# Attention over 4096 tokens: the denominators of a round and two output projections share one exchange of three PSUM banks at the 14th tile of keys

## The chip, the core and the metric

The kernel runs on one core of one Trainium2 chip, in one launch. The metric is the device time of an execution in microseconds (us); less is better. Engines are named as in the profile: PE is TensorE's matmul, PEld its weight load, DVE is VectorE, ACT is ScalarE, POOL is GpSimd, SP is SyncE (here it only issues DMAs). L1860 is line 1860 of the kernel before.

## What is computed

A small network on one image of 256 channels, 64 x 64 pixels: a convolution-like layer of windowed linear attention, then softmax attention over all 4096 pixels as tokens, then a mixture of 8 experts of which each token uses two. The change lies in the softmax attention:

```python
def _L1_attn_ref(x, w_qkv, b_qkv, w_out, b_out):
    b, n, d = x.shape                      # 1, 4096, 256
    h = 8; dh = d // h; scale = d ** (-0.5)
    q, k, v = split(x @ w_qkv + b_qkv)     # 8 heads of 32
    dots = jnp.einsum('bhid,bhjd->bhij', q, k) * scale
    attn = jax.nn.softmax(dots, axis=-1)
    out = jnp.einsum('bhij,bhjd->bhid', attn, v)
    return out @ w_out + b_out
...
t = t + _L1_attn_ref(_ln_t(t), ...)
t = t + _L1_ffn_ref(_ln_t(t), ...)         # logits, top 2 of 8, gelu experts
```

Everything is float32.

## The kernel before, in words

**Stages.** The first layer takes the span to about 960 us, the queries, keys and values to 1065, the attention stage to about 2163, the experts the rest, with the output at the end.

**The attention stage** works on transposed scores: keys lie on the 128 partitions, 512 queries along a row. A *round* r is one chunk of 512 queries (qc, 8 of them) and one group of four heads (g, 2 of them): 16 rounds, r = 0 to 15, the two groups of a chunk one after the other. A round goes over NT = 32 *tiles* i of 128 keys. One pass of the loop at L1982 is a *step*, one tile of one round:

- `scores` (L1848) makes the scores of four heads: the first head goes into a bank called "one" (a single buffer), heads 2 to 4 into a set of three banks called "three" (two buffers, L1814). [...] ScalarE takes the exponential of "one" (L1869) and then of "three" (L1872) into one of eight SBUF buffers of 4 x 512.
- `value_sums` (L1894) multiplies the weights of the tile two steps back by the values, summing over the round in "acc" (L1819, four heads side by side in the columns of the array). At the end of a round `take` copies the sums to the result (L1904).
- `add` (L1889) sums the exponentials of the tiles on VectorE (L1892), into the buffer of the round's first tile; every fourth tile from the sixth on is instead added to the second tile's buffer by an accumulating DMA on POOL's queue (`moved`, L1880). `gather` (tile 5 of the next round, L1912) joins the two sums.

Tiles are counted from 0 below and in the code, so the 14th tile is i = 13.

**The denominators** of round r-1 are handled during round r. `pack` (i = 9) takes a set of "three", sums the joined sums over the partitions by a multiplication with ones (L1919, recorded at L1819 with `ones` among its operands), and ScalarE copies the result to SBUF (L1922); SP writes four rows to DRAM (L1924) and reads them back spread over the partitions (L1925). `turn` (i = 17) takes reciprocals (L1932), writes them (L1933) and broadcasts each head's row to 32 partitions (four DMAs, L1936). `spread` (i = 29) multiplies the result of the round by them (L1943).

**The projections.** A tile of 128 tokens of the result is multiplied by w_out, together with 8 columns for the router's logits (L1794, 264 columns; `project`, L1791), added to the residual t by VectorE (L1798) and its mean and variance taken (L160, L161). `some_projections` (L1973) takes a set of "three" for two tiles. It is called at i = 13 and 25 of the rounds of the second group from round 3 on: 14 calls, 28 of 32 tiles; the last four come after the loop (L2022).

A use of a set of "three" by `pack` or `some_projections`, between the scores of two tiles, is called an *exchange* here.

**The early routing** of the first 12 tiles of tokens is cut into small VectorE operations with planned costs (L1088 to L1198). L1952 to L1968 distribute them over places (r, i) of rounds 8 to 14, each with so much room. Two of the pieces are matmuls: `count` (L1126) and `invert` (L1167). They use the third bank of an exchange of projections (`shared`, L1962) and are issued ahead of the projections; VectorE copies their results (L1130, L1177) after the additions of L1798.

**What sets the order.** The order in which things are written, readiness as the builder estimates it, and orders that are written by hand: `tc.issue_after(x)` puts an instruction behind x on its engine. ScalarE's copy in `pack` is behind the current exponential of "three" (L1921) and the next exponential is behind that copy (L1868). `work_on` (L2006) starts the loads of the first two experts at i = 0 and 29 of the last round, behind the last broadcast of `turn`. The list `free` (L1842) decides which of the eight buffers a tile gets: the one that is due free first, where `pack` frees the round's sum with due time NT(r + 1) + 11 (L1927).

Of the kernel before, what the change touches and what calls it, by code (L numbers as in the profile page):

```python
# [31 lines left out]
C = 256  # L32
KC = C // P
N = 4096
NT = N // P
# [5 lines left out]
NB = IMG // BH  # L41
# [5 lines left out]
NE = 8  # L47
# [73 lines left out]
def tile_conv_attn_hybrid(ctx: ExitStack, tc: tile.TileContext, a: dict, out: bass.AP):  # L121
# [62 lines left out]
    early = act[:, :, 3 * N // 4 : 3 * N // 4 + 3 * C + NE]  # L184
# [37 lines left out]
    def tok(i):  # L222
        return slice(P * i, P * (i + 1))
# [44 lines left out]
    with ExitStack() as phase:  # L268
# [406 lines left out]
        def packed(jobs):  # L675

            steps = []
            for job in jobs:
                if not steps or sum(j[0] for j in steps[-1]) + job[0] > CH:
                    steps.append([])  # L680
                steps[-1].append(job)
            return steps
# [359 lines left out]
    def all_of(ops):  # L1042
        for op in ops:
            op()
# [169 lines left out]
    with ExitStack() as phase:  # L1214
# [15 lines left out]
        with (  # L1230
# [55 lines left out]
            def turn(c):  # L1286
                for i in range(NB * c, NB * (c + 1)):
                    hn = work.tile([P, C], F32, name="hn", bufs=4) if c else first_rows(i)
                    if c:
                        norm.apply(hn, i)  # L1290
                    to_channels(hn, act[:, :, tok(i)], ps)

                    nc.gpsimd.tensor_add(t[:, i, :C], t[:, i, :C], bo)
# [497 lines left out]
        def project(prs, tiles, result, then=None):  # L1791
            for pr, i in zip(prs, tiles):
                for k in range(KC):
                    nc.tensor.matmul(  # L1794
                        pr[:, : C + NE], result(k, i), wo[:, k, :], start=k == 0, stop=k == KC - 1
                    )
            for pr, i in zip(prs, tiles):
                nc.vector.tensor_add(t[:, i, :], pr[:, : C + NE], t[:, i, :])  # L1798
            if then:
                then()  # L1800
            for i in tiles:
                found = norm2.stats(i)
            return found

        with tc.If(tame > 0) as branch:
            with (
# [6 lines left out]
                def three_banks():  # L1813
                    return ps.tile([P, 3, CH], F32, tag="three", name="ps_three", bufs=2)  # L1814
# [21 lines left out]
                result = lambda g, qc: act[:, 0, CH * (2 * g + qc % 2) : CH * (2 * g + qc % 2 + 1)]  # L1836
                buffers = [work.tile([P, 4 * CH], F32, name=f"pe{n}") for n in range(5)]
                buffers += [act[:, k, 4 * CH * n : 4 * CH * (n + 1)] for k, n in ((0, 1), (1, 0), (1, 1))]
                own, other = 0, 1
                by_dma = range(5, NT, 4)  # L1840
                head = lambda z, hd: z[:, CH * hd : CH * (hd + 1)]
                free = [(-1, n) for n in range(len(buffers))]  # L1842
# [3 lines left out]
                weights_of, acc_of, sums_of, emptied = {}, {}, {}, []  # L1846
# [42 lines left out]
                def add(r, i):  # L1889
                    if i not in (own, other) and not moved(r, i):  # L1890
                        total = buffers[sums_of[r, own]]
                        latest[:] = [nc.vector.tensor_add(total, total, weights_of[r, i]).ins]  # L1892

                def value_sums(r, i):  # L1894
                    (qc, g), pe = rounds[r], weights_of.pop((r, i))
                    if i == 0:
                        acc_of[r] = ps.tile([P, CH], F32, tag="acc", name="ps_acc")
                    values = lambda hd: v[:, i, P * g + D * hd : P * g + D * (hd + 1)]
                    per_head(acc_of[r], values, lambda hd: head(pe, hd), i == 0, i == NT - 1)
                    return pe  # L1900

                def take(r, copy):
                    qc, g = rounds[r]
                    return copy(result(g, qc), acc_of.pop(r))  # L1904

                def by_ones(to, weights, start, stop):
                    per_head(to, lambda hd: ones, lambda hd: head(weights, hd), start, stop)

                def gather(r):
                    total, moved_total = (buffers[sums_of[r, i]] for i in (own, other))  # L1910
                    with tc.issue_after(latest[0]):
                        nc.vector.tensor_add(total, total, moved_total)  # L1912
                    free.append((NT * (r + 1) + 8, sums_of[r, other]))

                held, latest, turned = [], [], []

                def pack(r):
                    den = three_banks()[:, 0]
                    by_ones(den, buffers[sums_of[r, own]], True, True)  # L1919
                    rec = work.tile([P, CH], F32, tag="rec", name="rec")  # L1920
                    with tc.issue_after(emptied[0]):  # L1921
                        emptied.append(nc.scalar.copy(rec, den).ins)  # L1922
                    some = work.tile([P, CH // D], F32, name="some")
                    nc.sync.dma_start(dens, rec[::D, :])  # L1924
                    nc.sync.dma_start(some, packed(dens))  # L1925
                    held.append(some)
                    free.append((NT * (r + 1) + 11, sums_of[r, own]))  # L1927

                def turn():
                    some = held.pop()  # L1930
# [9 lines left out]
                def spread(r):  # L1940
                    qc, g = rounds[r]
                    with tc.issue_after(latest[0]):
                        nc.vector.tensor_mul(result(g, qc), result(g, qc), held.pop())  # L1943

                last = len(rounds) - 1
                projected = []
# [4 lines left out]
                early, shared = {(8, 1): [load_early]}, {}  # L1951
                slots = [  # L1952
                    (r, i, room)
                    for r in range(8, len(rounds) - 1)
                    for i, room in ((1, 2.2), (9, 0.7), (13, 0.95), (17, 0.8), (21, 0.95), (25, 0.95))
                ]
                r, i, room = slots.pop(0)
                for cost, ops in pieces:
                    if cost is None:
                        while not (r % KC == KC - 1 and i in (13, 25)) or (r, i) in early:  # L1960
                            r, i, room = slots.pop(0)
                        shared[r, i] = ops  # L1962
                        r, i, room = slots.pop(0)
                        continue
                    if cost > room:
                        r, i, room = slots.pop(0)
                    room -= cost
                    early.setdefault((r, i), []).extend(ops)  # L1968
# [1 line left out]
                first_bank = lambda: ps.tile([P, CH], F32, tag="one", name="ps_one")  # L1970
                work_on = run(usual, slot_ps, beside, done, first_bank)

                def some_projections(n, also=None):  # L1973
                    tiles = list(range(len(projected), len(projected) + n))
                    projected.extend(tiles)
                    pr = three_banks()
                    then = also(pr[:, n]) if also else None
                    return project(
                        [pr[:, j] for j in range(n)], tiles, lambda k, i: result(k, i // NB)[:, tok(i % NB)], then
                    )  # L1980

                for s, (r, i) in enumerate(places):  # L1982
                    qc, g = rounds[r]
                    scores(r, i)
                    if s > 1:
                        value_sums(*places[s - 2])
                        if places[s - 2][1] == NT - 1:
                            behind = take(places[s - 2][0], nc.vector.tensor_copy)
                    if r and i == 5:
                        gather(r - 1)  # L1990
                    if r and i == 9:
                        pack(r - 1)
                    if r and i == 17:
                        turn()
                    if r and i == 29:
                        spread(r - 1)
                    if qc and g == KC - 1 and i in (13, 25):
                        behind = some_projections(2, shared.get((r, i)))
                    if s < len(places) - 2:
                        add(r, i)  # L2000
                    if (r, i) in early:
                        with tc.issue_after(latest[0]), tc.issue_after(behind.ins):
                            all_of(early[r, i])
                    if r == last and i in (0, NT - 3):
                        with tc.issue_after(turned[0]):
                            next(work_on)  # L2006

                den = three_banks()[:, 0]
# [11 lines left out]
                    nc.vector.reciprocal(rec[:, tok(n)], den[:, tok(n)])  # L2020
                    nc.vector.tensor_mul(to, to, rec[:, tok(n)])
                while len(projected) < NT:  # L2022
                    some_projections(2)
            route_and_run(work_on, slot_ps, beside, done)
        with branch.Else():


            with (
# [8 lines left out]
                for hd in range(2 * 4):  # L2037
                    g, hs = hd // 4, slice(D * (hd % 4), D * (hd % 4 + 1))
# [116 lines left out]
```

## Time and profile before

| | |
|---|---|
| median of three runs | 2713.83 us (2709.9 to 2714.03) |
| profiled execution | 2709.02 us |
| its span, first to last instruction | 2707.1 us |
| busy in the span: PE, DVE, ACT, POOL | 2624.4, 1880.5, 1518.1, 817.9 us |
| mean granted TensorE clock | 0.99 |
| scores (L1860), all rounds | 8192 matmul records, 612 ns each, many side by side |
| exponentials (L1872, L1869) | 1446 and 598 ns each, 512 of each |
| sums on VectorE (L1892) | 368 of 2292 ns |
| copy of the denominators (L1922) | 15 of 592 ns |
| additions after projections (L1798) | 424 ns each |

Busy times of PE overlap: four value sums or eight score matmuls run at the same time in different parts of the array, so starts tell more than durations. A float32 matmul leaves two records. In a group's row, "32x512 f32 x6144" is the output's shape and how many there are; in the timeline the first number is the start within the span, the second the time from the first start to the last end of the merged records, and a bracket shows how long the engine was idle before and what released it.

### The profile page before, as it was taken

The numbers are of one execution on the slowest core, as the hardware profiler recorded it, in microseconds if no ns is written. First come the engines' busy times: TensorE is split into PE (matmuls) and PEld (weight loads), VectorE is DVE, ScalarE is ACT, GpSimd is POOL, SyncE is SP. The second block draws the span as 40 slices with busy tenths as digits, with TensorE's granted clock in tenths as the row PEclk, the third lists the DMA queues.
The fourth block names the chain that finished last, engine by engine and source line by source line (L and its number), as shares of the span: only waits on it lengthen the run. The fifth ranks groups of instructions, "written<-read, shape, count | busy, mean of one in ns | idle before, by whom it ended". The sixth has DMA issues, their size and how long they took to land.

```text
span 2707.1 us, 70743 instructions
## 1 busy us (share of the span) xinstructions
PE 2624.4 (97%) x30398; PEld 1221.8 (45%) x30398; DVE 1880.5 (69%) x2570; ACT 1518.1 (56%) x2079; POOL 817.9 (30%) x919
## 2 busy tenths in 40 slices
PE   6999999999999999999999999999999999999995
PEld 5465436746544654111212121212121278888884
DVE  6868788586878866888888889888888871111114
ACT  3342323234232435999898989898989842222222
POOL 2067777306777731010000100000001122222220
PEclk9899999999999999999999999999999999999996
DMA  5000000000000000555555555555556645555555
GB/s 148 7 19 26 10 29 22 12 13 23 26 9 31 22 22 13 113 115 118 110 114 114 118 109 118 105 118 118 126 114 151 153 142 197 173 200 170 191 175 196
DMA packets 114461, 256.56 MB, mean 95 GB/s; under 512 B 19890, under 2 KB 76440, under 8 KB 100052
## 3 DMA queue, kind: packets, MB, share of 16 engines
q0 software_dynamic: 22240, 132.66, 23.4%
q1 hardware_dynamic: 84724, 110.30, 12.5%
q10 hardware_dynamic: 7168, 8.92, 1.0%
q8 instruction: 242, 3.96, 0.6%
q14 instruction: 87, 0.71, 0.1%
HBM read 118.64 MB, written 17.86 MB: 50 GB/s over the span
## 4 chain that ended last, share of the span: by engine, by line
PE 91%; DVE 4%; DMA 3%; issue 1%; ACT 1%; POOL 0%; ACTq 0%; SPq 0%; DVEq 0%; POOLq 0%
PE ps_three L1860 19%; PE ps_acc L1819 19%; PE ps_sc L887 8%; PE ps_yp L1528 8%; PE ps_hp L1511 7%; PE ps_acc L903 7%; PE ps_sc L767 3%; PE ps_sc L797 3%; PE ps_acc L841 3%; PE ps_two L441 2%; PE ps_mm L1303 2%; DMA yrows<-v,qk 2%; PE ps_two L534 1%; PE ps_acc L816 1%; PE ps_three L1794 1%; PE ps_mm L1318 1%
## 5 line engine op out<-in xcount | busy, mean ns | idle before, releaser
L1860 PE MATMUL ps_three<-qk 32*64 32x512 f32 x6144 | 563.2, 612 | 2.3 <-DVE t L1798 1.3
L1860 PE MATMUL ps_one<-qk 32*64 32x512 f32 x2048 | 556.3, 613 | 0.2 <-ACT pe L1869 0.2
L1892 DVE TENSOR_TENSOR act<-act,pe 128x2048 f32<-128x2048 f32 x195 | 447.3, 2294 | 82.5 <-ACT pe L1872 51.6
L1872 ACT ACTIVATE pe<-ps_three 128x1536 f32<-128x1536 f32 x330 | 477.3, 1446 | 0.0
L651 ACT COPY sm<-ps_sc 128x384 f32<-128x384 f32 (+2 forms) x418 | 212.9, 539 | 452.4 <-PE ps_sc L887 323.0
L659 DVE TENSOR_TENSOR sm<-ps_sc,mask 128x512 f32<-128x512 f32 (+3 forms) x788 | 343.3, 499 | 64.7 <-PE ps_sc L887 62.3
L659 POOL TENSOR_TENSOR sm<-sm,mask 128x192 f32<-128x192 f32 (+4 forms) x444 | 349.9, 819 | 113.3 <-ACT sm L651 113.2
L1892 DVE TENSOR_TENSOR act<-act 128x2048 f32<-128x2048 f32 x150 | 343.8, 2292 | 51.4 <-ACT act L1872 37.9
L1880 POOL DMA_DIRECT2D pe<-pe x108 | 93.4, 865 | 939.8 <-ACT pe L1872 610.4
L1819 PE MATMUL ps_acc<-pe,v 128*32 128x512 f32 x2640 | 351.6, 604 | 0.0
L1514 ACT ACTIVATE v<-ps_hp,qk 128x256 f32<-128x256 f32 (+1 forms) x256 | 123.1, 481 | 342.6 <-PE ps_hp L1511 342.6
L1860 PEld LDWEIGHTS ps_three<-qk 32*64 32x64 f32 x6144 | 112.6, 129 | 414.5 <-ACT pe L1869 244.0
L1872 ACT ACTIVATE act<-ps_three 128x1536 f32<-128x1536 f32 x182 | 263.1, 1446 | 0.0
L1528 PE MATMUL ps_yp<-qk,v 128*128 128x256 f32 (+1 forms) x1088 | 241.7, 380 | 0.0
L1511 PE MATMUL ps_hp<-qk 128*128 128x256 f32 (+1 forms) x1024 | 236.8, 389 | 2.8 <-ACT v L1514 1.7
L887 PE MATMUL ps_sc<-qk 32*128 32x256 f32 (+5 forms) x3456 | 233.2, 445 | 0.1
L1869 ACT ACTIVATE pe<-ps_one 128x512 f32<-128x512 f32 x330 | 197.5, 598 | 58.3 <-PE ps_one L1860 33.8
L1528 PEld LDWEIGHTS ps_yp<-qk,v 128*128 128x128 f32 (+1 forms) x1088 | 200.3, 187 | 30.7 <-issue 1.3
L903 PE MATMUL ps_acc<-sm,v 128*32 128x256 f32 (+4 forms) x2816 | 211.7, 407 | 0.1
L659 POOL TENSOR_TENSOR sm<-sm,ycut 128x512 f32<-128x512 f32 (+3 forms) x130 | 144.4, 1133 | 214.0 <-ACT sm L651 213.7
L1511 PEld LDWEIGHTS ps_hp<-qk 128*128 128x128 f32 x1024 | 180.7, 189 | 52.7 <-ACT v L1514 12.8
L1819 PE MATMUL ps_acc<-act,v 128*32 128x512 f32 x1456 | 193.9, 604 | 0.0
(364 smaller groups left out, 2908.8 us busy)
## 6 DMA issues: line engine op xcount, KB each, us to landing
pe<-pe POOLq DMA_DIRECT2D x108, 1024.0 KB, 7.6
qk<-in_L_ffn_W SPq DMA_DIRECT2D x64, 1024.0 KB
by<-recs SPq DMA_DIRECT2D x48, 256.0 KB
rows<-in_x SPq DMA_DIRECT2D x16, 256.0 KB
qk<-in_L_ffn_b SPq DMA_DIRECT2D x32, 128.0 KB
y<-yrows SPq DMA_DIRECT2D x8, 512.0 KB
y<-yrows ACTq DMA_DIRECT2D x8, 512.0 KB
rec<-recs SPq DMA_DIRECT2D x60, 64.0 KB
```

Source lines behind the costliest of these rows:

```text
L651: copied = nc.scalar.copy(sm[:, :used], sc[:, :used])
L659: done = engine.tensor_mul(to, of, mk.unsqueeze(1).to_broadcast(list(to.shape)))
L887: nc.tensor.matmul(scs[h][u : u + rows, at : at + n], kT[hs[h], P * i + u : P * i + u + rows], qT[hs[h], CH * ix + CELL * c0 : CH * ix + C ...
L903: nc.tensor.matmul(acc[hs[h], CELL * c0 : CELL * c1], v[:, i, hs[h]], sms[h][:, at : at + n], start=not begun[0], stop=last and at == plac ...
L1511: nc.tensor.matmul(hp[:, :n], w1[:, k, tok(m)], x_now[:, k, :n], start=k == 0, stop=k == KC - 1)
L1514: done["gelu"] = nc.scalar.activation(hid[:, m, :n], hp[:, :n], AF.Gelu, bias=cols[:, m : m + 1]).ins
L1528: product = nc.tensor.matmul(yp[:n], hid[:, m, P * j : P * j + n], w2[:, m, :], start=m == 0, stop=m == NH - 1)
L1819: nc.tensor.matmul(to[D * hd : D * (hd + 1), :], lhsT(hd), rhs(hd), start=start, stop=stop, skip_group_check=True,)
L1860: nc.tensor.matmul(to[CELL * u : CELL * (u + 1), :], qk[hs, 1, g, P * i + CELL * u : P * i + CELL * (u + 1)], qk[hs, 0, g, chunk(qc)], sta ...
L1869: first = nc.scalar.activation(head(pe, 0), one, AF.Exp, scale=C**-0.5)
L1872: nc.scalar.activation(pe[:, CH:], three.rearrange("p h n -> p (h n)"), AF.Exp, scale=C**-0.5).ins
L1892: latest[:] = [nc.vector.tensor_add(total, total, weights_of[r, i]).ins]
```

## The change

Five things move; no operation on data is added or left out.

- `pack` goes from i = 9 to i = 13 and no longer takes a set of banks itself: it gets the first bank of a set that the loop takes.
- From round 3 on, the loop issues two projections in the second and third bank of the same set, in every round and right after `pack`. The calls at i = 13 and 25 of the second group's rounds go; one call at i = 25 of the last round is left, with a set of its own.
- `turn` goes from i = 17 to i = 21; `spread` stays at i = 29. The sum's buffer is due free at NT(r + 1) + 15 instead of + 11.
- `count` and `invert` use the columns past 264 in the bank of the first of the two projections. They are written after the additions of L1798 instead of before the projections, and may be at i = 13 of any round.
- The early routing begins at i = 17 of round 8 instead of i = 1, and the rooms of its places change.

```diff
-                def pack(r):
-                    den = three_banks()[:, 0]
+                def pack(r, den):
                     by_ones(den, buffers[sums_of[r, own]], True, True)
...
-                    free.append((NT * (r + 1) + 11, sums_of[r, own]))
+                    free.append((NT * (r + 1) + 15, sums_of[r, own]))
...
-                    for i, room in ((1, 2.2), (9, 0.7), (13, 0.95), (17, 0.8), (21, 0.95), (25, 0.95))
+                    for i, room in ((1, 2.2), (9, 0.95), (13, 0.7), (17, 0.95), (21, 0.8), (25, 0.95))
+                    if r > 8 or i > 13
...
-                        while not (r % KC == KC - 1 and i in (13, 25)) or (r, i) in early:
+                        while i != 13 or (r, i) in early:
...
-                def some_projections(n, also=None):
-                    tiles = list(range(len(projected), len(projected) + n))
+                def some_projections(prs, also=None):
+                    tiles = list(range(len(projected), len(projected) + len(prs)))
                     projected.extend(tiles)
+                    then = (lambda: also(prs[0][:, C + NE :])()) if also else None
+                    return project(prs, tiles, lambda k, i: result(k, i // NB)[:, tok(i % NB)], then)
+
+                def two_projections():
                     pr = three_banks()
-                    then = also(pr[:, n]) if also else None
-                    return project(
-                        [pr[:, j] for j in range(n)], tiles, lambda k, i: result(k, i // NB)[:, tok(i % NB)], then
-                    )
+                    return some_projections([pr[:, j] for j in range(2)])
...
-                    if r and i == 9:
-                        pack(r - 1)
-                    if r and i == 17:
+                    if r and i == 13:
+                        pr = three_banks()
+                        pack(r - 1, pr[:, 0])
+                        if r > KC:
+                            behind = some_projections([pr[:, j] for j in (1, 2)], shared.get((r, i)))
+                    if r and i == 21:
                         turn()
...
-                    if qc and g == KC - 1 and i in (13, 25):
-                        behind = some_projections(2, shared.get((r, i)))
+                    if r == last and i == 25:
+                        behind = two_projections()
...
                 while len(projected) < NT:
-                    some_projections(2)
+                    two_projections()
```

## The prediction, made before the change was run

> **What bounds the kernel now.** I read the slices of the span, then the busy time of single rounds, then TensorE's timeline inside a round, then the waits of the attention stage.
>
> ```profile
> PE   6999999999999999999999999999999999999995
> DVE  6868788586878866888888889888888871111114
> ACT  3342323234232435999898989898989842222222
> ```
>
> From 1065 to 2156 us (slices 17 to 32, the attention stage, the only one that the change edits) TensorE and ScalarE are both full and VectorE nearly so. Next, the busy times of rounds 4 to 7 (stretch, length, PE, PEld, DVE, ACT); rounds 5 and 7 project four tiles each, rounds 4 and 6 none.
>
> ```profile
> 1333.30:1399.90 66.60, 66.60 (x780) 12.93 (x776) 56.33 (x28) 62.60 (x66) 6.03 (x7) 1.00 0.57 116
> 1399.90:1470.40 70.50, 70.50 (x796) 15.81 (x792) 59.43 (x40) 62.56 (x66) 6.28 (x9) 1.00 0.54 110
> 1470.40:1536.90 66.50, 66.50 (x780) 12.89 (x776) 56.30 (x28) 62.57 (x66) 6.03 (x7) 1.00 0.56 114
> 1536.90:1607.30 70.40, 70.40 (x796) 15.78 (x792) 59.81 (x40) 62.55 (x65) 7.50 (x8) 1.00 0.57 116
> ```
>
> PE fills each round; ScalarE has 4 to 8 us to spare in it. Two pairs of projections make a round 3.95 us longer: **one pair costs 1.98 us**. A plain step (one tile of keys) takes 2.04 us between the starts of the exponentials of L1869, 32 of them 65.28: **one denominator costs 66.5 - 65.28 = 1.22 us**. What these consist of shows in the timeline, first of the denominator at the 10th tile of round 5 (start, length):
>
> ```profile
> 1416.90 0.67 PE L1860 MATMUL ps_three<-qk 32*64 32x512 f32 x6
> ...
> 1417.94 1.06 PE L1819 MATMUL ps_acc<-act,v 128*32 128x512 f32 x8
> ...
> 1418.71 1.45 ACT L1872 ACTIVATE pe<-ps_three 128x1536 f32<-128x1536 f32 x1
> 1418.82 1.04 PE L1819 MATMUL ps_three<-act,ones 128*32 128x512 f32 x8
> ...
> 1419.80 0.64 PE L1860 MATMUL ps_one<-qk 32*64 32x512 f32 x1
> ...
> 1420.05 0.59 ACT L1922 COPY rec<-ps_three 128x512 f32<-128x512 f32 x1
> ...
> 1420.22 0.68 PE L1860 MATMUL ps_three<-qk 32*64 32x512 f32 x6
> ```
>
> The denominator occupies one of the two sets of three banks, so the scores of the next tile need the other set, which ScalarE still reads until 1418.71 + 1.45 = 1420.16. PE could go on at 1419.80 and does so at 1420.22. Work of the denominator: 1419.80 - 1416.90 - 2.04 = 0.86 us; the rest of the 1.22, 0.36 us, is this stall. Then the projections at the 14th tile:
>
> ```profile
> 1428.24 2.29 DVE L1892 TENSOR_TENSOR act<-act,pe 128x2048 f32<-128x2048 f32 x1
> ...
> 1428.37 2.05 PE L1794 MATMUL ps_three<-wo,act 128*128 128x264 f32 x8
> ...
> 1430.35 0.67 PE L1860 MATMUL ps_three<-qk 32*64 32x512 f32 x6
> ...
> 1430.46 0.77 DVE L1798 TENSOR_TENSOR t<-ps_three,t 128x264 f32<-128x264 f32 x2
> ```
>
> 1430.35 - 1428.37 = 1.98 us, all of it work: these matmuls last longer than ScalarE's read, and VectorE's two additions end at 1431.2, before the banks are wanted at 1432.4. The waits of the stage (us in total, times, longest) agree; they know few others on this pair of buffers:
>
> ```profile
> PEld ps_three L1860 <- ACT pe L1872: 4.3, 16, 1.1
> ...
> PEld ps_three L1860 <- DVE t L1798: 2.2, 1, 2.2
> ```
>
> **What the Trainium skill says.** "PSUM — Partial Sum Buffer", section "PSUM bank collisions raise a hardware error": two engines must not touch one bank and quadrant at a time, whichever columns they take, so they are kept apart by bank. The trace agrees where two engines read one tile: VectorE's copy of L454 waited 16.8 us (12 times) for ScalarE's L453, though both only read. So the denominator (first bank) doesn't bar the projections (second and third bank), but the counts, which move from a bank of their own into the bank of a projection, must wait for VectorE's addition. The same page, section "Engine vs sequencer instructions": matmuls start and complete in program order, so a waiting one holds all behind it. The trace fits: at 1419.80 one matmul went ahead, all others stood until 1420.22.
>
> **The change, part by part.**
> - *Thirteen denominators (rounds 3 to 15) share their exchange with a pair of projections.* Before, 1.22 + 1.98 = 3.20 us apart. After, scores, values, denominator, projections follow each other; by the time the next scores want the other set, 2.90 + 1.98 = 4.88 us have passed since the last scores began, and ScalarE's read has long ended (3.25 us: 1428.13 + 1.45 - 1426.33): no stall. 0.86 + 1.98 = 2.84 us. Saved: 0.36 x 13 = 4.7 us. ScalarE's copy (0.59 us) falls into its idle time (it idled 2.05 us at the projections of before). VectorE's sum of the 13th tile ends 4.2 us after those scores began (1430.53 - 1426.33), before the matmuls do at 4.9; the additions end near 5.7 and the banks are wanted at 6.9. Cover gone, each us late costs one us.
> - *Rounds 1 and 2, and the pair at the 26th tile of round 15:* same operations, 1.22 and 1.98 us as before. The 1.3 us that PE lost to L1798 in that last one stays.
> - *Pairs spread over rounds.* 14 pairs in both, 4 tiles left for the end in both; each chunk's results are final before use. 0.
> - *Counts after the additions.* 4 small matmuls (0.48 us) and 24 (1.47 us, 1839.91 to 1841.38) are as many as before. New is the wait for the addition, 0.04 + 0.43 us plus a hop: at most 0.65 us each if PE stands, 0 if the next scores are put ahead. Both: 0 to 1.3; I take 0.4, since the order on an engine follows estimated readiness (the matmul at 1419.80 was pulled ahead of six that are written before it).
> - *Denominator four tiles later, turn four later.* The sums' buffer comes free 4 tiles later, so buffers are reused one step tighter at tiles 10 to 17. VectorE's sums end 2.8 us or more before the exponential that overwrites (starts of L1869 against ends of L1892, all rounds); the denominator's 1.2 us at tile 9 leaves this cover, still over 1.5 us. The moved tile 5 lands at most 9.7 us after issue, about 12 us are there. 0. On SP's queue the two DMAs of pack and the five of turn go past the row stores of L1186 and, in round 15, hold the weight loads of L1441 back 8 us (2136.6 before); those rows are first multiplied at 2185.6 and had landed by 2164: 0. On POOL's queue none of the moved steps issues anything. From the issue of L1933 the broadcast's last packets end 9.3 to 14.7 us later; the multiplication of L1943 was 24.2 later, now four steps less, 16.1. Cover 1.4 us, and behind it VectorE's 2.8: 0, and if a landing were 5 us later, about 1 us each time.
> - *Early routing* starts at tile 17 of round 8 instead of tile 1 and ends in round 13 instead of 12, two rounds before its lists are needed: 0.
>
> Sum: -4.7 + 0.4 = **-4.3 us**. On the profiled execution (2709.02 us, span 2707.1) that is 2704.7. The median of the runs is 2713.83, 0.18% above it; carried to it: **2709.5 us**, -0.16%.
>
> **Rivals.**
> 1. *The stall is only moved: no change.* At 1842.07 VectorE was free and the first of two projections was done at 1842.5, yet L1798 began at 1843.45, with the second. So a read of one bank waited for the write of another: the three banks may be tracked as one. Then the projections count as later than ScalarE's copy of the denominator, and the builder, which orders by readiness, can put the next scores ahead of them; these stall 0.36 as before. For it, that wait and the matmul of 1419.80; against it, the page's rule by bank. 2713.83 + 0.4 = 2714.
> 2. *Slower.* The same tracking, but the projections stay in front on PE. The copy comes after the exponential of three banks and ends 1420.64 - 1416.90 = 3.74 us after the scores, against 2.90 when PE is ready: with a hop 0.9 us of waiting each time. 13 x (0.9 - 0.36) = +7.0, with 0.4: 2721.3. It decides from 0.36 us of waiting per exchange. Against it speaks that PE's order gives way.
> 3. *More than forecast:* counts free and the full PE stall of 0.42 saved, 13 x 0.42 = 5.5 us: 2708.3.
>
> **Chances.** A measurement of this kernel tells about 0.2% (5.4 us) from no change; 2708.4 and 2719.3 are the bounds. Forecast 0.50 (of which 0.13 ends beyond 0.2% by the scatter of the runs, 2709.9 to 2714.03); rival 1 0.25; rival 2 0.13; rival 3 0.12 (all but 0.01 of it counted faster). Faster 0.13 + 0.11 = 0.24; slower 0.13 and 0.01 from rival 1's scatter = 0.14; the same 0.62. The forecast's own range is 2706.5 to 2712.5; with rivals 1 and 3 and the scatter 2705 to 2716, which leaves out rival 2 and some tails.
>
> **What would show it.** In the profile after: rounds 3 to 15 of about 68.1 us each (65.28 + 2.84), the last longer by its extra pair; PE passing from L1819 (ones) to L1794 after 0.98 us; no wait of L1860 on L1872 except in rounds 1 and 2; L1943 at most a fraction of a us late. Wrong would be scores between L1819 (ones) and L1794, or PE standing before L1794 until ScalarE's copy has ended, or L1860 waiting for L1798.

## The result, and the profile after

| | before | after |
|---|---|---|
| median of 22 runs each on one chip, us | 2712.05 (2707.42 to 2725.34) | 2724.82 (2716.87 to 2732.09) |
| ratio, 95% interval | | 1.0037 [1.0025, 1.0049] |
| profiled execution, us (span) | 2709.02 (2707.1) | 2725.55 (2723.7) |
| span until the attention stage starts (first exponential of the single bank) | 1064.9 | 1069.8 |
| attention stage (from that start to the last one of its kind) | 1091.8 | 1103.6 |
| span after it | 550.4 | 550.3 |

The kernel became slower by 0.37%, about 10 us. The ratio compares fast runs with fast runs and is not the quotient of the two medians, which is 1.0047. In the two profiled executions the attention stage is 11.8 us longer; the 4.9 us ahead of it lie in stages that the change leaves alone (last section). So from here on rounds are compared, not whole spans.

The slices of the span look as before, with every engine as full as it was: averages do not show a loss of this kind.

```profile
PE   6999999999999999999999999999999999999995
DVE  6968788576878866888888888888888871111114
ACT  3342323233232435999999999989899842222222
```

The busy times of rounds 4 to 7 do show it (same columns as in the prediction: stretch, length, PE, PEld, DVE, ACT):

```profile
1337.20:1406.40 69.20, 69.20 (x792) 14.35 (x784) 57.98 (x34) 62.60 (x66) 6.02 (x7) 1.00 0.55 111
1406.40:1475.50 69.10, 69.10 (x788) 14.34 (x784) 57.99 (x34) 62.58 (x66) 6.26 (x9) 1.00 0.55 112
1475.50:1544.60 69.10, 69.10 (x788) 14.37 (x784) 57.94 (x34) 62.52 (x66) 6.02 (x7) 1.00 0.54 109
1544.60:1613.70 69.10, 69.10 (x788) 14.35 (x784) 58.27 (x34) 62.49 (x66) 7.48 (x8) 1.00 0.55 114
```

The 1.00 towards the end of a line is the granted clock; it was 1.00 in these rounds before, too. Rounds 3 to 14 now have one pair of projections each, so all are alike but the two with counts. The mean of before was (66.5 + 70.5) / 2 = 68.5 us; it is 69.1 us now, and the forecast was 68.1. With 32 plain steps at 65.28 us, the shared exchange costs 69.1 - 65.28 = **3.82 us**, against 3.20 us apart before and 2.84 us forecast: 1.0 us is lost in each. TensorE's and ScalarE's timeline in round 5 shows where (start, length):

```profile
1433.03 1.45 ACT L1872 ACTIVATE act<-ps_three 128x1536 f32<-128x1536 f32 x1
1433.14 1.04 PE L1819 MATMUL ps_three<-act,ones 128*32 128x512 f32 x8
...
1434.11 1.07 PE L1860 MATMUL ps_one<-qk 32*64 32x512 f32 x2
1434.36 0.59 ACT L1921 COPY rec<-ps_three 128x512 f32<-128x512 f32 x1
1435.11 1.63 PEld L1794 LDWEIGHTS ps_three<-wo,act 128*128 128x128 f32 x8 [0.81 <-ACT rec L1921]
1435.11 2.05 PE L1794 MATMUL ps_three<-wo,act 128*128 128x264 f32 x8
1437.09 0.67 PE L1860 MATMUL ps_three<-qk 32*64 32x512 f32 x6
```

The ones are through at 1434.11 and the projections do not follow until 1435.11. Between stands one score matmul of the next tile, one of the two into the single bank (the program issues eight per tile and the trace shows sixteen, so x2 is one instruction). ScalarE's copy of the denominator (L1921, it was L1922 before) ends at 1434.95, just ahead of the projections. Two things lie in that 1.0 us, a wait for the copy and a matmul put in front, and TensorE looks busy all through it. The waits of the stage name the copy. Of the lines of before on L1860, the one on L1872 has shrunk from 4.3 to 1.4 us; the one on L1798 (round 15) stays:

```profile
DVE t L1798 <- PE ps_three L1794: 20.5, 13, 1.8
...
PEld ps_three L1794 <- ACT rec L1921: 10.5, 13, 0.8
...
PEld ps_three L1860 <- DVE t L1798: 1.9, 1, 1.9
PEld ps_three L1860 <- ACT pe L1872: 1.4, 2, 1.1
```

Thirteen waits of L1794 for L1921 are one for each shared exchange. Behind a denominator L1860 waits for L1872 in rounds 1 and 2 alone (0.2 us each in PEld's account; the 1.1 us is the start of the stage), as forecast: the stall that was to be saved was saved, and a longer one came in its place.

The two exchanges with counts lose more. Round 10, at `count`:

```profile
1780.64 2.05 PE L1794 MATMUL ps_three<-wo,act 128*128 128x264 f32 x8
1782.62 1.08 PE L1860 MATMUL ps_three<-qk 32*64 32x512 f32 x6
1782.79 0.77 DVE L1798 TENSOR_TENSOR t<-ps_three,t 128x264 f32<-128x264 f32 x2 [1.77 <-PE ps_three L1794]
1783.63 0.65 PE L1129 MATMUL ps_three<-qk 128*128 128x48 f32 x4
1784.20 0.65 PE L1860 MATMUL ps_three<-qk 32*64 32x512 f32 x3
```

The count matmuls (two, in four records) start when VectorE's two additions are done (1782.79 + 0.77 = 1783.56). Three of the next tile's score matmuls (six records) were put in front, and the rest follow the counts.

### The profile page after: what moved, and what is told of

Its sections match the earlier page's. It is cut to its first block, busy times and chain, and to the rows that moved or that the text cites. A ratio compares the mean times of both kernels' runs of the same rounds, so it can differ in the third digit from the quotient of the medians.

```text
span 2723.7 us, 70750 instructions
## 1 busy us (share of the span) xinstructions
PE 2642.4 (97%) x30398; PEld 1226.6 (45%) x30398; DVE 1880.7 (69%) x2570; ACT 1516.9 (56%) x2079; POOL 816.7 (30%) x919
## 5 line engine op out<-in xcount | busy, mean ns | idle before, releaser
L1860 PE MATMUL ps_three<-qk 32*64 32x512 f32 x6144 | 566.0, 613 | 2.0 <-DVE t L1798 1.0
L1860 PE MATMUL ps_one<-qk 32*64 32x512 f32 x2048 | 565.1, 613 | 0.2 <-ACT pe L1869 0.2
L1872 ACT ACTIVATE pe<-ps_three 128x1536 f32<-128x1536 f32 x290 | 419.6, 1447 | 0.0
L1880 POOL DMA_DIRECT2D pe<-pe x100 | 86.3, 863 | 893.0 <-ACT pe L1872 652.6
L1872 ACT ACTIVATE act<-ps_three 128x1536 f32<-128x1536 f32 x222 | 321.0, 1446 | 0.0
L1819 PE MATMUL ps_acc<-pe,v 128*32 128x512 f32 x2320 | 309.8, 606 | 0.0
L1860 PEld LDWEIGHTS ps_three<-qk 32*64 32x64 f32 x6144 | 113.0, 130 | 423.3 <-ACT pe L1869 229.7
L1892 DVE TENSOR_TENSOR act<-act 128x2048 f32<-128x2048 f32 x105 | 240.6, 2292 | 39.8 <-ACT act L1872 23.1
L1892 DVE TENSOR_TENSOR act<-act,pe 128x2048 f32<-128x2048 f32 x102 | 233.8, 2292 | 31.5 <-ACT pe L1872 21.1
L1892 DVE TENSOR_TENSOR pe<-pe,act 128x2048 f32<-128x2048 f32 x97 | 222.3, 2292 | 40.8 <-ACT act L1872 30.8
L1819 PE MATMUL ps_acc<-act,v 128*32 128x512 f32 x1776 | 236.5, 604 | 0.0
```

Source lines behind the costliest of these rows:

```text
L1819: nc.tensor.matmul(to[D * hd : D * (hd + 1), :], lhsT(hd), rhs(hd), start=start, stop=stop, skip_group_check=True,)
L1860: nc.tensor.matmul(to[CELL * u : CELL * (u + 1), :], qk[hs, 1, g, P * i + CELL * u : P * i + CELL * (u + 1)], qk[hs, 0, g, chunk(qc)], sta ...
L1872: nc.scalar.activation(pe[:, CH:], three.rearrange("p h n -> p (h n)"), AF.Exp, scale=C**-0.5).ins
L1880: moving = nc.gpsimd.dma_start(buffers[sums_of[r, other]], pe, accum_op=ALU.add)
```

## The experiments

Theory A: the set of three banks is tracked as one tile. What TensorE writes into it after another engine's read, in the order of the program, waits for that read, though it goes to another bank: the projections for ScalarE's copy, the counts for VectorE's additions. Theory B: the longer exchange itself costs the time, and the copy is only what is last seen. The runs on theory C, which came up on the way, follow.

All times of rounds come from the starts of the exponentials of the single bank. "Twelve rounds" are rounds 3 to 14, with twelve pairs of projections and both count exchanges in every kernel. Each ratio is to runs of the kernel before on the same chip.

| kernel | plain shared round, us | twelve rounds, us | against before, us | ratio to before, 95% interval |
|---|---|---|---|---|
| before | 66.5 and 70.5 | 824.0 | | |
| after | 69.1 | 835.0 | +11.0 | 1.0037 [1.0025, 1.0049] |
| e1_reads_last | 68.1 | 822.6 | -1.4 | 0.9997 [0.9985, 1.0009] |
| e2_counts_first | 68.1 | 819.2 | -4.8 | 0.9974 [0.9962, 0.9986] |
| e3_copy_twice | 69.6 | 839.1 | +15.1 | 1.0050 [1.0035, 1.0064] |
| e4_den_in_one | 68.1 | 823.6 | -0.5 | 0.9994 [0.9983, 1.0004] |
| e5_own_sets | 69.1 | 833.4 | +9.4 | 1.0035 [1.0023, 1.0047] |
| e6_last_pair_earlier | 68.1 | 819.2 | -4.8 | 0.9964 [0.9949, 0.9979] |
| e7_held_one_set | 69.0 | 833.4 | +9.4 | 1.0047 [1.0025, 1.0070] |
| e8_held_own_sets | 68.5 | 826.2 | +2.1 | 1.0007 [0.9996, 1.0017] |

**e1_reads_last.** The projections are written ahead of ScalarE's copy and VectorE's additions; nothing else changes. `pack` returns its second half, and `project` calls it between its matmuls and its additions:

```diff
                     by_ones(den, buffers[sums_of[r, own]], True, True)
-                    rec = work.tile([P, CH], F32, tag="rec", name="rec")
-                    with tc.issue_after(emptied[0]):
-                        emptied.append(nc.scalar.copy(rec, den).ins)
...
+                    def read():
+                        rec = work.tile([P, CH], F32, tag="rec", name="rec")
+                        with tc.issue_after(emptied[0]):
+                            emptied.append(nc.scalar.copy(rec, den).ins)
...
+                    return read
...
+            if reads:
+                reads()
             for pr, i in zip(prs, tiles):
                 nc.vector.tensor_add(t[:, i, :], pr[:, : C + NE], t[:, i, :])
```

> The change, but in a shared exchange all multiplications (ones and the two projections) are written before any engine reads the set: ScalarE's copy of the denominators and VectorE's additions come after. Theory A (the set of three banks is tracked as one, so that projections written after ScalarE's copy wait for it): the wait of about 1.0 us in each of 13 rounds goes, plain merged rounds fall from 69.1 to 68.1 us (65.28 + 0.86 + 1.98), PE passes from L1819 with ones to L1794 without a hole; 13 us less than the change, about 0.1% under the kernel before (the counts still wait in rounds 10 and 12). Theory B (the longer exchange itself costs it: changes of shape, matmuls put in between, engines that cool down; the copy is only the last thing that the profile sees): rounds stay within 0.3 us of 69.1 and the time within 3 us of the change, 1.003 of the kernel before.

Measured: 68.1 us a round. TensorE's timeline in round 5 (L1821 and L1862 are L1819 and L1860 of the changed kernel):

```profile
1430.91 1.04 PE L1821 MATMUL ps_three<-act,ones 128*32 128x512 f32 x8
1431.89 2.05 PE L1794 MATMUL ps_three<-wo,act 128*128 128x264 f32 x8
1433.86 0.67 PE L1862 MATMUL ps_three<-qk 32*64 32x512 f32 x6
```

The ones pass to the projections after 0.98 us, and these to the scores after 1.97: the picture that the prediction had drawn, with its 2.84 us. The exchange does the same work as in the changed kernel, so theory B falls. What the rounds gain, the counts eat up: round 10 took 2.1 us and round 12 3.1 us more than the others.

The waits have not vanished; they have moved to the readers:

```profile
ACT rec L1925 <- PE ps_three L1794: 22.7, 13, 1.8
...
DVE t L1800 <- ACT rec L1925: 13.8, 13, 1.3
```

ScalarE's copy, which reads the first bank, now waits for the projections into the other two, and VectorE's additions, which read those two, wait for ScalarE's copy. Here that costs nothing, as the 68.1 us show. It is also a second view of theory A: whichever comes later in the program waits, even a read for a read.

**e2_counts_first.** As e1, with the counts too ahead of both reads:

```diff
+                    def between():
+                        if also:
+                            counts.append(also(prs[0][:, C + NE :]))
+                        if reads:
+                            reads()
```

> As the kernel with all reads last, and the counts of the early routing (4 matmuls in round 10, 24 in round 12) also stand before every read of the set. Theory A: their wait for VectorE's addition goes too; round 10 falls from 70.7 - 1.0 to 68.1 + 0.45 = 68.6 us, round 12 from 73.3 - 1.0 to 68.1 + 1.5 = 69.6 us; in all some 3 us less than with the reads last alone, 4 to 5 us under the kernel before (0.998). Theory B: rounds 10 and 12 keep 1.5 and 4 us above their neighbours, whatever the order.

Measured: rounds 10 and 12 are 0.38 and 1.48 us above the others, which is about the length of the counts' own matmuls. Round 10:

```profile
1775.69 2.05 PE L1794 MATMUL ps_three<-wo,act 128*128 128x264 f32 x8
...
1777.58 0.54 PE L1129 MATMUL ps_three<-qk 128*128 128x48 f32 x4
...
1778.05 0.67 PE L1862 MATMUL ps_three<-qk 32*64 32x512 f32 x6
```

No wait is left on TensorE in the exchange; ScalarE's and VectorE's waits stay as in e1. In e1 the two waits had cost 1.75 + 1.67 = 3.4 us. In the changed kernel round 10 loses 1.57 - 0.38 = 1.2 us, and round 12 about as much (2.60 - 1.48 = 1.1 us in e5, where the clock did not fall): 2.3 us. This kernel is faster than the one before, by 0.26%.

**e3_copy_twice.** The changed kernel with the suspected wait made longer:

```diff
+                        copied = nc.scalar.copy(rec, den)
+                    with tc.issue_after(copied.ins):
                         emptied.append(nc.scalar.copy(rec, den).ins)
```

> The change, with ScalarE's copy of the denominators made twice in a row into the same place (the result is that of the change). ScalarE idles 3.4 us there, so the second copy costs nothing by itself. Theory A: projections wait for the second copy, 0.5 us more in each of 13 rounds: merged rounds 69.6 us, 6 to 7 us above the change, 1.006 of the kernel before. Theory B: as the change, 1.0035 to 1.004.

Measured: 69.57 us, 0.47 longer for 0.59 us more of ScalarE. The projections do wait for the end of the copies, and in the changed kernel that wait is about 0.1 us shorter than what stands on TensorE meanwhile. The rounds show this, not the totals: 1.0050 fell short of the 1.006 of theory A, and its interval overlaps that of the changed kernel.

**e4_den_in_one.** The denominators that are handled in rounds 3 to 15 go to the single bank, so that they share no tile with the projections; the writing order is that of the change:

```diff
-                        pack(r - 1, pr[:, 0])
+                        pack(r - 1, ps.tile([P, CH], F32, tag="one", name="ps_one") if r > KC else pr[:, 0])
```

> The change, with the order of writing kept (ScalarE's copy before the projections), but from round 3 on the denominators stand in the single bank 'one', which is a tile of its own, and the projections alone in the set of three. Theory A: no common tile, no wait; merged rounds 68.1 us as with the reads last, about 0.1% under the kernel before; the next scores of the first head find 'one' free, since the copy ends 3.8 us after the last scores began and they come at 4.9. If any read of PSUM by ScalarE held the projections back, or under theory B: 69.1 us and 1.003.

Measured: 68.1 us, with the projections 0.99 us after the ones began. Without a common tile there is no wait, whatever the order. But here, as in e1, no score matmul stands between them either, so the two things in the 1.0 us are still not told apart.

**e5_own_sets.** The merge is undone in place: denominator and projections take a set each.

```diff
-                        pr = three_banks()
-                        pack(r - 1, pr[:, 0])
+                        pack(r - 1, three_banks()[:, 0])
                         if r > KC:
+                            pr = three_banks()
```

> The change with its merge undone and its position kept: the denominators take a set of three banks of their own, and the projections right after them take another. Theory A (the projections wait for ScalarE's copy only because both lie in one set): the projections follow the ones and the one single-bank matmul without a wait for the copy, and the set that they need is one the exps have left, or they wait for that exp; a merged round falls from 69.1 us to about 65.28 + 1.22 + 1.98 = 68.5 us, since the 0.36 us stall of a denominator with its own set stays. Over the stage 13 times 0.6 = 8 us less than the changed kernel; the two count exchanges keep their 3 us, so about 1.001 of the kernel before. Theory B (the exchange is simply longer at this position): still 69.1 us a round and about 1.004.

Measured: 69.1 us, where theory A had 68.5. A miss for theory A, but e1 had already spoken against theory B. Round 5:

```profile
1432.58 1.45 ACT L1872 ACTIVATE act<-ps_three 128x1536 f32<-128x1536 f32 x1
1432.69 1.04 PE L1819 MATMUL ps_three<-act,ones 128*32 128x512 f32 x8
...
1433.66 1.07 PE L1860 MATMUL ps_one<-qk 32*64 32x512 f32 x2
1433.91 0.59 ACT L1921 COPY rec<-ps_three 128x512 f32<-128x512 f32 x1
...
1434.66 2.05 PE L1794 MATMUL ps_three<-wo,act 128*128 128x264 f32 x8
```

The projections need the set that the exponential leaves at 1432.58 + 1.45 = 1434.03, and they begin at 1434.66, when the lone score matmul is through. That matmul alone is enough for the 1.0 us. Hence a theory C: in the changed kernel too the lone matmul costs the time, and the copy's wait lies under it. The trace can't decide it: here too it names the copy as what released L1794, and the copy ends at 1434.50, 0.16 us ahead of the projections.

**e7_held_one_set** and **e8_held_own_sets** settle that: the changed kernel and e5, each with the scores and values of the next tile held behind the projections on TensorE, so that nothing can stand in front of them.

```diff
-                    nc.tensor.matmul(
+                    wrote = nc.tensor.matmul(
                         pr[:, : C + NE], result(k, i), wo[:, k, :], start=k == 0, stop=k == KC - 1
                     )
+            ahead[:] = [wrote.ins]
...
                         for u in range(2):
-                            nc.tensor.matmul(
+                            with tc.issue_after(ahead[0]) if i == 14 and ahead else nullcontext():
+                                nc.tensor.matmul(
...
-                        value_sums(*places[s - 2])
+                        with tc.issue_after(ahead[0]) if i == 14 and ahead else nullcontext():
+                            value_sums(*places[s - 2])
```

> The changed kernel, with the 15th tile's scores and the values beside them held behind the projections on TensorE, so that no score matmul runs between the ones and the projections (in the changed kernel one, of the single bank, does, and occupies TensorE for 0.99 us). Theory A (the wait for ScalarE's copy costs the time; the lone score matmul only fills the wait): the projections start when the copy has ended, 0 to 0.1 us earlier than now, and merged rounds stay at 69.0 to 69.1 us; about 1.003 of the kernel before. Theory C (the lone score matmul itself costs it, and the copy's wait is only covered by it): the projections follow the ones at once and merged rounds fall to 68.1 us; about 0.9995.

> The kernel in which the projections have a set of three banks of their own (69.1 us a merged round, although its projections do not lie in the set that the copy reads), with the same scores held behind the projections. Both theories: the projections then wait only for the exponential of their set, which ends about 0.37 us after the ones, so a merged round is 65.28 + 0.86 + 1.98 + 0.4 = 68.5 us, and the lone score matmul cost 0.55 us in it; about 1.001 of the kernel before. If it stays at 69.1 us, what held the projections there was neither the score matmul nor the exponential, and the copy bars them even across sets.

Measured: 69.0 and 68.5 us. In round 5 of e7 (the first two lines are TensorE's, the third ScalarE's):

```profile
1432.51 1.04 PE L1822 MATMUL ps_three<-act,ones 128*32 128x512 f32 x8
1434.37 2.05 PE L1796 MATMUL ps_three<-wo,act 128*128 128x264 f32 x8 [0.83 <-ACT rec L1925]
...
1433.73 0.59 ACT L1925 COPY rec<-ps_three 128x512 f32<-128x512 f32 x1
```

and of e8:

```profile
1430.07 1.04 PE L1822 MATMUL ps_three<-act,ones 128*32 128x512 f32 x8
1431.45 2.05 PE L1796 MATMUL ps_three<-wo,act 128*128 128x264 f32 x8 [0.35 <-ACT act L1876]
...
1429.96 1.44 ACT L1876 ACTIVATE act<-ps_three 128x1536 f32<-128x1536 f32 x1
1431.29 0.59 ACT L1925 COPY rec<-ps_three 128x512 f32<-128x512 f32 x1
```

With one set TensorE now stands idle for 0.83 us, until 0.05 us after the copy's end (1433.73 + 0.59 = 1434.32). With two sets it waits 0.35 us, until 0.05 us after the exponential's end (1431.40), and the projections run while ScalarE still copies (until 1431.88): a copy out of another set does not bar them. So theory A holds for the changed kernel: without the lone matmul its rounds are only 0.13 us shorter. The lone matmul fills a wait there; in e5 it cost 69.1 - 68.5 = 0.6 us of its own.

**e6_last_pair_earlier.** e2, with the pair at tile 25 of round 15 moved to tile 21:

```diff
-                    if r == last and i == 25:
+                    if r == last and i == 21:
```

> The kernel with all of TensorE's writes ahead of the reads, counts included, and the last pair of projections of round 15 at tile 21 instead of tile 25. In the kernel without this edit round 15 took 69.4 us, with one wait of 1.3 us of the next scores for VectorE's additions, which stood behind other work of VectorE. Theory A: that wait is VectorE's backlog at tile 25, so at tile 21 it goes and round 15 falls to about 68.1 us; total about 0.997 of the kernel before. Theory B: the wait belongs to any pair late in round 15, so round 15 stays at 69.4 us and the total at 0.9975.

Measured: round 15 fell from 69.4 to 68.1 us, and L1862 waits for no addition there any more. In e2 the additions of that pair stood behind VectorE's sums of the keys' tiles, which ended at 2149.15, while the projections were through at 2146.51. At 0.9964 [0.9949, 0.9979] e6 has the lowest ratio of this study, but its interval overlaps that of e2; the gain of the last step rests on the 1.3 us of round 15.

## Why the prediction was wrong, point by point

The forecast was 2709.5 us (2705 to 2716), most likely no measurable change; it came out slower, outside the range. Rival 2, at a chance of 0.13, had the mechanism. Two of the signs of being wrong that the prediction names came true: a score between the ones and the projections, and, with that score held back (e7), TensorE standing until the copy has ended.

- **The step that failed:** "So the denominator (first bank) doesn't bar the projections (second and third bank)". It was drawn from the rule by bank in the Trainium skill, "PSUM — Partial Sum Buffer", section "PSUM bank collisions raise a hardware error". That rule says what two engines must keep apart; it does not say that the program holds no other waits. Here the waits follow the tile of three banks: e1 (order alone) and e4 (another tile alone) each remove the 1.0 us, and e7 shows TensorE standing 0.83 us for the copy. The wait cited for the rule, L454 for L453, fits both readings, since each of the two reads goes over both banks of its tile. The evidence against it was in the trace of before and is told under rival 1: L1798 waited for the second projection when the first was ready. A wait seen in the kernel's own trace should have outweighed a rule about the chip, and a forecast by the tile would have begun with 0.9 us of waiting, not with none.
- **"0.86 + 1.98 = 2.84 us"** for a shared exchange: right in e1, e2, e4 and e6 (68.1 - 65.28 = 2.8). It holds where the writes come first or the denominator has a tile of its own. In the changed kernel it is 3.82.
- **"Saved: 0.36 x 13 = 4.7 us":** the old stall did go. The 1.0 us in its place makes 0.62 x 13 = 8 us of loss.
- **ScalarE's copy "falls into its idle time":** so it does, and costs ScalarE nothing; but TensorE waits for it. Hidden on its own engine is not hidden from those who wait.
- **The counts, +0.4, bounds 0 to 1.3:** mis-sized, about 2.2 us for both (they add 4.2 us to their two rounds, with round 12 taken from e5, against 2.0 before). The bound took 0.65 us each, for the tail of the additions. But VectorE begins the first addition only when both projections are done, so 0.9 us pass from the end of the projections to that of the additions, and the scores put in front don't shorten what follows: three took 1.0 us until the counts, and the rest of the tile another 1.0 after them. (The prediction's "4 small matmuls" are four records of two.)
- **The order on TensorE.** The forecast held that scores are pulled ahead where a wait is expected. They were, but only one of eight, into the single bank; rival 1's "no change" needed all of them in front.
- **VectorE's additions before the banks are wanted:** right. No wait of L1860 for L1798 but the one in round 15 (1.0 us on PE, 1.3 before), about as the prediction said; e6 shows that it goes with the pair's place.
- **Rounds 1 and 2, the moved `pack` and `turn`, buffers, SP's queue:** right at 0. Rounds 1 and 2 took 66.50 us in both kernels. The broadcast's last packets ended 7.5 to 14.7 us after issue, and the multiplication (L1942 now) began after 15.9 us or more, without a wait. The span after the stage, where late weight loads would show, is 550.3 us against 550.4.
- **Early routing later:** right at 0; rounds 8, 13 and 14 are like the others.
- **Rival 2's price:** 0.9 us of waiting, 2721.3 us. The wait was 0.83 (e7) and, with the lone matmul in it, 1.0 us.

The sum for the twelve rounds: 12 x (69.10 - 68.51) = 7.1 us, where 68.51 is the mean of the rounds of before without counts; the counts 2.2; and a spell of lower clock in round 12 of this execution 1.6 (the round took 4.24 us more than the others, in e5 without such a spell 2.60): 10.9 us, of 11.0 seen.

## What to carry to other kernels

- Before a merge of two steps into one buffer, ask in which order the program writes and reads it: a write that comes after another engine's read can wait for it even in another bank. Put all writes ahead of the first read; here that order alone turned 1.0037 into 0.9974 (e2). The reads then wait for the writes, and for each other, so look whether the reading engines have room for it.
- A busy engine can hide a wait: look at what is done in the gap, and whether doing it there makes anything later shorter. To tell a wait from what fills it, hold the filler back, as in e7 and e8.
- Where the kernel's trace and a rule disagree on what waits for what, follow the trace.

## What the runs showed of the hardware that was not expected

**A lone matmul of 32 rows, ahead of one of full height, costs TensorE as much as eight.** In e5 one score instruction took 1.07 us, 1.0 until the projections, which use all 128 rows. The other seven of the tile then took 1.04 us (1436.63 to 1437.67), as long as all eight in the next step (1438.67 to 1439.71):

```profile
1436.63 0.67 PE L1860 MATMUL ps_three<-qk 32*64 32x512 f32 x6
...
1437.67 1.07 PE L1819 MATMUL ps_acc<-pe,v 128*32 128x512 f32 x8
1438.67 0.67 PE L1860 MATMUL ps_three<-qk 32*64 32x512 f32 x6
...
1439.71 1.07 PE L1819 MATMUL ps_acc<-act,v 128*32 128x512 f32 x8
```

The Trainium skill, "TensorE: Matmul & The Clock Gate", section "Part 3: Packing small matmuls — row/col tiling", says that matmuls at different tile positions of the array run concurrently; the trace agrees (eight instructions are through in 1.04 us, where one takes 1.0). What follows from it here is that pulling one of such a group forward, ahead of a matmul of full height, saved nothing later.

**The granted clock falls to half for short spells, at other places in other executions.** In the changed kernel's profile one of 13.65 us lay at about 598 us, ahead of everything that the change touches; the later start of the attention stage (4.9 us) is put down to it, which was not tried. It fits that VectorE's instructions, matched one by one with those of before, run 2.3 us ahead at 558 us and 4.1 us behind at 647 us. Another followed `invert` in round 12 (the column after the busy times is the granted clock):

```profile
1926.00:1929.60 3.60, 3.60 (x28) 0.53 (x24) 1.16 (x1) 1.94 (x2) 0.00 (x0) 0.57 0.13 21
```

Round 12 was some 1.6 us longer with it. The profiles of e4 and e7 have a spell there too, those of the kernel before, e1, e2, e3, e5, e6 and e8 do not. With one profile each, it stays open whether the wait at `invert` brings it on.
